# Column products three steps apart and spline ramps two steps apart, in work that runs beside a convolution

## The chip, the cores and the metric

The kernel runs on one core of a Trainium2 chip. The metric is the device time of one execution in microseconds; a kernel's time is the median of several runs. Five engines matter: TensorE (PE, matrix products into PSUM), ScalarE (ACT), VectorE (DVE), GpSimd (POOL) and SyncE (SP), which here only issues transfers between HBM and the core's memory (SBUF). Each engine works through its own instructions in the order in which the program gives them, and semaphores hold an instruction until what it needs is there.

## What is computed

The input x has shape 8 x 64 x 128 x 128, in float32. Four layers follow each other, each after a group norm and each added to its input:

```python
x = x + L0(gn(x))   # adder convolution 3x3: relu(b - sum |patch - w|)
x = x + L1(gn(x))   # per element: scale_base * silu + scale_sp * cubic B-spline + bias
x = x + L2(gn(x))   # Haar transform, depthwise 3x3, pointwise, 3x3, gelu, inverse Haar
x = x + L3(gn(x))   # nearest of 512 embedding vectors per pixel
```

Layer 0 costs most: for each of 64 output channels the absolute difference of every input channel and tap is formed and summed over 64 channels and 9 taps. Group norm needs a whole image before the next layer can begin.

## The kernel before

Images are worked on in pairs: 2 images x 64 channels fill the 128 partitions. There are four pairs. **Layer 0** (`layer0`) of a pair is 4 chunks of 32 rows x 4 groups of 16 output channels, 16 passes; each pass has 16 x 9 = 144 *taps*. A tap is one of three things. ScalarE forms |x - w| for a whole chunk (L821, 128 x 4096 elements). Or VectorE forms a maximum (L774), which gives the absolute difference with terms added elsewhere. Or VectorE fuses a second maximum into the same buffer (L844). TensorE then sums the buffer over the channels with 8 matmuls of 512 columns (L809), and the buffer is free again. There are seven narrow buffers, and beside the other layers two wide ones that also hold the padded input.

The order is written out ahead by a planner, when the program is built. It keeps a clock for each engine, adds a fixed cost for each instruction (`COSTS`, `ABS`, `MAX`, `FUSED`, `SUM`), and always issues what can start first. The number of taps for each engine in a pass follows from its clocks.

**Beside** layer 0 of the pairs 1, 2 and 3 run layers 1, 2 and 3 of the pair before (`layer1_beside`, `layer2_beside`, `layer3_beside`). They are cut into *steps*. `STEPS` gives how many steps each layer has (208, 500, 24 for the first statistics of a later pair, 396), 1128 in all for a pair's 16 x 144 = 2304 taps, so that a step comes about every second tap. `at(step, f, ...)` lists what is issued in which step; within a step the order is that of the listing. The planner knows what these pieces cost, but no waits between them. Layers 1 to 3 of the last pair run alone at the end; the change does not touch them.

**Layer 1 beside** takes 16 chunks a pair, one in 12 steps. For each of three knots p and two images i: a ramp (`ramp_on_act`, ScalarE, L1340, for three of the six; else `ramp`, VectorE, L1345), its square (ScalarE, L1349) and its cube (VectorE, L1353), then `products` (TensorE, L1368, 8 matmuls) of both images. Ramps have two buffers, squares and cubes three (`r3`), used in turn: a ramp waits until the cube two before has read its buffer, a square until the products have read the buffer of three before. `silu`, `base`, `right` (L1377) and `total` (L1381, L1382) end a chunk. With the chunk's first step b and s = b + 1 + 4p, the ramps of both images are in step s, the squares in s + 1, the cubes in s + 2, the products in s + 4.

**Layer 2 beside** takes 8 chunks a pair, one in 56 steps. Four *kinds* of column products m follow each other. `columns_of` (VectorE, L1496) makes the input `v`; four *bursts* of 12 matmuls (`products`, TensorE, L1511) fill `mm`; a *take* moves `mm` out of PSUM into even and odd columns of `g`. The tiles `v`, `mm` and `g` have one buffer each. Each burst has its own weights, `u2`, 384 KB, loaded by SP (`load_u2`) into one buffer: the load can go when the burst before has read the buffer. SP issues this load among others: rows of x (L1451, L1558), results (L1574, L673). `gelu` (ScalarE, L1551), `inverse` (TensorE, L1564), `add` (VectorE, L1569) and `store` follow.

With b the chunk's first step, kind m has `columns_of` in step b + 11m, its bursts in b + 11m + 3, 5, 7 and 9, its take in b + 11m + 11. GELU is in b + 46, the inverse products in b + 48, 49, 57 and 58. The takes are:

```python
first:  ScalarE  even = mm               # kind 0
second: VectorE  even += mm              # kind 1, L1536
        ScalarE  odd   = mm              #         L1537
third:  VectorE  even += mm; odd -= mm   # kind 2, L1542, L1543
fourth: VectorE  odd  -= mm              # kind 3, L1547
```

In the second take both engines write the same tile `g`, and the copy waits for the addition.

Of the kernel before, what the change touches and what calls it, by code (L numbers as in the profile page):

```python
# [16 lines left out]
ALU = mybir.AluOpType  # L17
# [22 lines left out]
PADDED = (RA + 2) * (W + 2)  # L40
ALONE = (9, 3, 9.0, 9.0, 11.0, 54)
BESIDE = (7, 99, 7.0, 8.0, 10.0, 40)
STEPS = (208, 500, 24, 396)
ABS_ALONE = [60] * NP
ABS_BESIDE = [66, 66, 66, 70, 73, 74, 74, 74, 74, 72, 68, 66, 66, 66, 66, 66] * 3
FIRST_MAX = 3
# [22 lines left out]
    "layer2_beside.border": {"DVE": 0.4},  # L69
    "layer2_beside.columns_of": {"DVE": 1.42},  # L70
    "layer2_beside.products": {"PE": 2.95},
    "layer2_beside.take_first": {"ACT": 1.0},
    "layer2_beside.take_second": {"DVE": 1.18, "ACT": 1.0},
    "layer2_beside.take_third": {"DVE": 2.36},
    "layer2_beside.take_fourth": {"DVE": 1.18},
    "layer2_beside.gelu": {"ACT": 1.05},
# [22 lines left out]
class Net:  # L99
# [1191 lines left out]
    def layer1_beside(self, pair, stats_in, stats, steps):  # L1291

        nc, tc = self.nc, self.tc
# [5 lines left out]
        def at(step, f, *a):  # L1299
            events[step].append((f, *a))  # L1300

        with ExitStack() as ctx:
# [89 lines left out]
            for n in range(2 * NCH):  # L1392
                b = 12 + EACH * n
                for i in range(2):
                    at(b - 2, load, n, i)
                    at(b, magnitude, n, i)
                at(b - 1, load_x, n)
                for p in range(NQ // 2):
                    s = b + 1 + 4 * p
                    for i in range(2):  # L1400
                        at(s, ramp_on_act if p < 1 + i else ramp, n, p, i)
                        at(s + 1, square, n, p, i)
                        at(s + 2, cube, n, p, i)
                    at(s + 4, products, n, p)
                at(b + 5, silu, n)
                at(b + 9, base, n)
                at(b + 14, right, n)
                at(b + 15, total, n)
            yield from self.spread_out(events, steps)

    def layer2_beside(self, stats_in, stats, steps):
# [3 lines left out]
        nc, tc = self.nc, self.tc  # L1415
# [6 lines left out]
        def at(step, f, *a):  # L1422
            events[step].append((f, *a))

        with ExitStack() as ctx:
# [96 lines left out]
            def even_and_odd(c):  # L1522
                g = gs[c].rearrange("p o i r (w b) -> p b i o (r w)", b=2)
                return g[:, 0], g[:, 1]

            def product_of(c, m):
                return mms.pop((c, m)).rearrange("p i o r w -> p i o (r w)")

            def take_first(c):
                gs[c] = sp.tile([P, 2, 2, G, S], F32, name="g")  # L1530
                nc.scalar.copy(even_and_odd(c)[0], product_of(c, 0))

            def take_second(c):
                even, odd = even_and_odd(c)
                ps = product_of(c, 1)
                nc.vector.tensor_tensor(even, even, ps, ALU.add)  # L1536
                nc.scalar.copy(odd, ps)  # L1537

            def take_third(c):
                even, odd = even_and_odd(c)  # L1540
# [38 lines left out]
            for j in range(NCH + 1):  # L1579
                b, each = (7, LEAD) if j == 0 else (7 + LEAD + EACH * (j - 1), EACH)  # L1580
                if j < NCH:
                    lo, row = (2 * G * j + 4, 2) if j else (0, 0)
                    hi = min(2 * G * (j + 1) + 4, H)
                    for h, s in enumerate((-5, -2, 1, 4) if j else range(0, 10, 2)):
                        to = min(lo + G // 2, hi)
                        if lo == to:
                            continue
                        at(max(b + s - 3, 0), load, j, h, lo, to)
                        at(b + s + 1, columns, j, h, to - lo)
                        if h == 0 and j > 0:  # L1590
                            at(b + s + 2, halo, j)
                        at(b + s + 2, rows, j, h, to - lo, row)
                        row += (to - lo) // 2
                        lo = to
                    for n in range(36):
                        at(b + 7 + n * (each - 10) // 36 if j else b + 11 + n * (each - 14) // 36, depthwise, j, n)
                    at(b + each - 2, border, j)
                if j >= 1:
                    c = j - 1
                    when = [(b + 11 * m + 3 + 2 * n, c, m, n // 2, n % 2) for m in range(4) for n in range(4)]  # L1600
                    for n, (step, *what) in enumerate(when):
                        at(when[n - 1][0] + 1 if n else b - 3, load_u2, *what)
                        at(step, products, *what)
                    for m, take in enumerate((take_first, take_second, take_third, take_fourth)):
                        at(b + 11 * m, columns_of, c, m)
                        at(b + 11 * m + 11, take, c)
                    for oab in range(2):
                        at(b + 46, gelu, c, oab)
                    for a in range(2):
                        s = b + 48 + 9 * a  # L1610
                        at(s - (8 if a == 0 else 1), load_x, c, a, 0)
                        for n in range(2):
                            at(s + n, inverse, c, 2 * a + n)
                        for h in range(2):
                            for n in range(2):
                                at(s + 3 + 4 * h, add, c, 2 * a + n, h)
                            at(s + 3 + 4 * h, store, c, a, h)
                        at(s + 4, load_x, c, a, 1)
# [101 lines left out]
    def run(self):  # L1720
# [5 lines left out]
        def raw(pair):  # L1726
            mrs[pair] = self.mr_tile()
            return self.raw_norm(pair, mrs[pair])

        def beside():  # L1730
            for pair in range(last):
                later = self.stats_tile("later")
                yield from self.layer1_beside(pair, stats.pop(pair), later, STEPS[0])
                between = self.stats_tile("between")
                yield from self.layer2_beside(later, between, STEPS[1])
                if pair + 1 == last:
                    self.load_early(last)
                if pair + 2 <= last:
                    yield from self.padded(raw(pair + 2), STEPS[2])
                yield from self.layer3_beside(between, pair, STEPS[3])  # L1740

        self.layer0([0], mrs, stats, ALONE, ABS_ALONE, [0] * (NP - 2) + [STEPS[2], 1], self.padded(raw(1), STEPS[2]))
        counts = []
        for pair in range(1, last + 1):
            total = sum(STEPS) + (1 - STEPS[2] if pair == last else 0)
            lead = 0 if pair == 1 else 20
# [49 lines left out]
```

## Time and profile before

| what | value |
| --- | --- |
| median of 3 runs | 18329.01 us (18328.6 to 18329.49) |
| profiled execution | 18391.41 us |
| its span | 18389.7 us |
| granted clock of TensorE, mean | 0.985 |
| busy: PE, DVE, ACT, POOL | 97%, 96%, 93%, 18% |
| layer 0 of the first pair, alone | about 0 to 3600 us |
| the three stretches beside layer 0: layer 1 | 3640 to 4545, 8280 to 9170, 12840 to 13725 us |
| layer 2 | 4545 to 6580, 9170 to 11150, 13725 to 15720 us |
| layer 3 | 6690 to 8200, 11260 to 12750, 15770 to 17270 us |
| layers 1 to 3 of the last pair, alone | about 17390 us to the end |

The profiled execution is 62 us longer than the median of the runs, so a sum over its rows is a difference that is then carried to the median. A row of the profile names a line of the code, an engine, an operation, the tile written and the tiles read; `r` stands for the ramps and for `r3` alike, `u` for `u2` and for the `u` of layer 1 (numbers in names are left out). A wait is written as "who <- for whom: total, how often, the longest", in us. PE busy times are modelled at their ends; idle gaps of an engine under 150 ns are not listed as waits. Each of the program's matmuls stands as two records.

### The profile page before, as it was taken

How to read it: one execution, taken by the hardware profiler on the slowest of the kernel's cores; microseconds unless marked ns; L12 is line 12 of the kernel's file. 1: busy time of each engine (PE TensorE's matmuls, PEld its weight loads, DVE VectorE, ACT ScalarE, POOL GpSimd, SP SyncE). 2: the span in 40 equal slices, each digit the busy share in tenths (PEclk: the TensorE clock that was granted, in tenths of full speed). 3: DMA queues.
4: the chain of work that ended last, by engine and by line, in shares of the span. 5: the costliest groups of instructions: out<-in, count | busy, mean ns of one | idle time of the engine just before them, and what ended most of it. 6: DMA issues, size and time to landing. Idle time of an engine off the chain costs nothing.

```text
span 18389.7 us, 338059 instructions
## 1 busy us (share of the span) xinstructions
PE 17822.3 (97%) x150418; PEld 6142.1 (33%) x150418; DVE 17676.9 (96%) x13410; ACT 17162.3 (93%) x6556; POOL 3386.7 (18%) x1866
## 2 busy tenths in 40 slices
PE   8999999999999999999999999999999999999998
PEld 2222222222333323332233333233223333222364
DVE  8999999999999999999999999999999999999887
ACT  7999999999999999999999999999999999999924
POOL 1222222200000024430000002443000000344205
PEclk9999999999999999999999999999999999999997
DMA  7767777611111111011111111101111111110231
GB/s 146 132 124 137 132 130 137 130 40 40 43 48 49 44 39 26 23 31 38 41 41 48 53 43 39 29 23 29 42 39 44 45 53 43 28 28 21 66 107 42
DMA packets 454213, 1099.90 MB, mean 60 GB/s; under 512 B 72416, under 2 KB 234848, under 8 KB 395360
## 3 DMA queue, kind: packets, MB, share of 16 engines
q0 software_dynamic: 111792, 491.89, 15.2%
q1 hardware_dynamic: 340960, 586.39, 11.2%
q8 instruction: 1178, 19.30, 0.4%
q14 instruction: 283, 2.32, 0.0%
HBM read 526.58 MB, written 125.74 MB: 35 GB/s over the span
## 4 chain that ended last, share of the span: by engine, by line
PE 54%; DVE 26%; issue 11%; ACT 6%; DMA 2%; POOL 1%; SPq 0%; DVEq 0%; another core or an unknown queue 0%; ACTq 0%; POOLq 0%
PE ps L809 41%; DVE buf L774 13%; ACT buf L821 4%; PE mm L1511 4%; DVE buf L844 4%; PE pd L1666 2%; DVE r L1353 1%; DVE wide L774 1%; PE ps L1227 1%; PE m L1079 1%; DMA u<-u_dram 1%; DVE dw L1484 1%; DVE nd L1678 1%; DVE x L774 1%; PE pa L953 0%
## 5 line engine op out<-in xcount | busy, mean ns | idle before, releaser
L809 PE MATMUL ps<-buf,sel 128*32 128x512 f32 x112848 | 12574.1, 595 | 168.4 <-ACT buf L821 87.6
L821 ACT ACTIVATE buf<-wide,w 128x4096 f32<-128x4096 f32 x1901 | 6922.4, 3711 | 80.1 <-PE ps L809 79.3
L821 ACT ACTIVATE buf<-x,w 128x4096 f32<-128x4096 f32 x1823 | 6647.1, 3711 | 129.3 <-PE ps L809 123.6
L809 PEld LDWEIGHTS ps<-buf,sel 128*32 128x32 f32 x112848 | 3540.5, 110 | 8634.0 <-issue 7801.0
L774 DVE TENSOR_SCALAR buf<-x,w 128x4096 f32<-128x4096 f32 x1801 | 4166.2, 2357 | 75.2 <-PE ps L809 68.8
L774 DVE TENSOR_SCALAR buf<-wide,w 128x4096 f32<-128x4096 f32 x1731 | 4028.8, 2367 | 95.3 <-PE ps L809 89.7
L1681 POOL DMA_INDIRECT g<-in_L_conv_embed_weight,ix x768 | 1860.2, 2422 | 2390.0 <-issue 1170.8
L844 DVE SCALAR_TENSOR_TENSOR buf<-x,w,buf 128x4096 f32<-128x4096 f32 x440 | 1973.3, 4485 | 15.7
L658 POOL DMA_DIRECT2D y<-in_x x496 | 704.9, 2173 | 6961.4 <-ACT y L645 5343.3
L844 DVE SCALAR_TENSOR_TENSOR buf<-wide,w,buf 128x4096 f32<-128x4096 f32 x430 | 1928.4, 4485 | 15.3
L1511 PE MATMUL mm<-v,u 64*128 64x256 f32 x9216 | 1182.0, 401 | 142.1 <-DMA u<-u_dram 129.1
L1511 PEld LDWEIGHTS mm<-v,u 64*128 64x128 f32 x9216 | 893.4, 195 | 557.4 <-issue 239.3
L832 POOL DMA_DIRECT2D buf<-buf x203 | 508.0, 2503 | 2739.6 <-DVE buf L774 2363.2
L821 ACT ACTIVATE x<-wide,w 128x4096 f32<-128x4096 f32 x263 | 975.9, 3711 | 5.8 <-PE ps L809 5.8
L821 ACT ACTIVATE wide<-x,w 128x4096 f32<-128x4096 f32 x259 | 961.1, 3711 | 4.8 <-PE ps L809 4.8
L809 PE MATMUL ps<-wide,sel 128*32 128x512 f32 x7696 | 923.1, 594 | 11.4 <-ACT wide L821 4.6
L809 PE MATMUL ps<-x,sel 128*32 128x512 f32 x7776 | 927.2, 593 | 3.3 <-ACT x L821 1.9
L1484 DVE SCALAR_TENSOR_TENSOR dw<-sub,dws,dw 128x512 f32<-128x512 f32 (+2 forms) x768 | 573.4, 747 | 10.4
L1668 ACT ACTIVATE t<-emb,xsq 128x512 f32<-128x512 f32 x768 | 512.2, 718 | 42.3 <-DVE xsq L1659 23.8
L1678 DVE CUSTOM_DVE_ANT_0 nd<-pd,t 128x512 f32<-128x512 f32 x768 | 519.6, 677 | 32.5 <-ACT t L1668 17.0
L774 DVE TENSOR_SCALAR x<-wide,w 128x4096 f32<-128x4096 f32 x223 | 529.5, 2374 | 8.9 <-PE ps L809 8.8
L1680 DVE FIND_INDEX8 ix<-best,nd 128x8 uint32<-128x512 f32 x768 | 526.2, 685 | 0.0
(288 smaller groups left out, 10465.5 us busy)
## 6 DMA issues: line engine op xcount, KB each, us to landing
buf<-buf POOLq DMA_DIRECT2D x203, 2048.0 KB
u<-u_dram SPq DMA_DIRECT2D x512, 384.0 KB
z<-x_dram SPq DMA_DIRECT2D x192, 256.0 KB
x<-x_dram SPq DMA_DIRECT2D x96, 512.0 KB
raw<-in_x SPq DMA_DIRECT2D x32, 1024.0 KB
x_dram<-y SPq DMA_DIRECT2D x512, 64.0 KB
y<-in_x POOLq DMA_DIRECT2D x496, 64.0 KB
x_dram<-x SPq DMA_DIRECT2D x48, 512.0 KB
```

The lines of the kernel that those rows point to most:

```text
L658: nc.gpsimd.dma_start(out=ys[p][at], in_=d, accum_op=ALU.add)
L774: nc.vector.tensor_scalar(ab, tap(p // OG, t), w[:, t : t + 1], None, ALU.max)
L809: nc.tensor.matmul(to, sel[:, M - 1 - m : 3 * M - 1 - m], rhs, start=(done % TAPS == 0), stop=((done + span) % TAPS == 0))
L821: nc.scalar.activation(ab, tap(p // OG, t), AF.Abs, bias=w[:, t : t + 1], scale=-1.0)
L832: nc.gpsimd.dma_start(out=into, in_=of, accum_op=ALU.add, max_dma_last_dim=8192)
L844: nc.vector.scalar_tensor_tensor(ab, tap(p // OG, t), w[:, t : t + 1], ab, ALU.max, ALU.add)
L1484: nc.vector.scalar_tensor_tensor(out, v, wt, out, ALU.mult, ALU.add)
L1511: nc.tensor.matmul(ps[:, i], u2[r, k % 2, di, :], vs[c, m][r, k, di : di + G, :], start=(k == 0 and di == 0), stop=(k == 3 and di == 2))
L1668: nc.scalar.activation(t, emb[:, 1], AF.Identity, bias=xsqs[j][:, n : n + 1])
L1678: nc.vector.tensor_tensor_reduce(nd, ps, t, 1.0, -FAR, ALU.subtract, ALU.max, mx[:, 0:1])
L1680: nc.vector.max_index(ix, mx, nd)
L1681: nc.gpsimd.indirect_dma_start(out=g[:, img, :], out_offset=None, in_=self.embed, in_offset=bass.IndirectOffsetOnAxis(ap=ix[:, 0:1], axis=0),)
```

## The change

In layer 1 beside, the ramps, squares and cubes of the second image are issued two steps after those of the first, and the cube two steps after its square; the products come in step s + 7. What ends a chunk comes three steps later. In layer 2 beside, the bursts stand three steps apart and the kinds 14 steps; a take is in the 15th step after its `columns_of`. Kind 1 is worked on first, and its take is two copies by ScalarE, into even and odd columns; kind 0 is second and only adds to the even columns. GELU and what follows move to b + 58 and b + 60. The steps of a chunk stay 12 and 56. The step counts grow from 208 to 212 and from 500 to 514, so that 1146 steps fall on the same 2304 taps. Buffers are as before.

```diff
-STEPS = (208, 500, 24, 396)
+STEPS = (212, 514, 24, 396)
...
-    "layer2_beside.take_first": {"ACT": 1.0},
-    "layer2_beside.take_second": {"DVE": 1.18, "ACT": 1.0},
+    "layer2_beside.take_first": {"ACT": 2.0},
+    "layer2_beside.take_second": {"DVE": 1.18},
...
                 for p in range(NQ // 2):
                     s = b + 1 + 4 * p
                     for i in range(2):
-                        at(s, ramp_on_act if p < 1 + i else ramp, n, p, i)
-                        at(s + 1, square, n, p, i)
-                        at(s + 2, cube, n, p, i)
-                    at(s + 4, products, n, p)
-                at(b + 5, silu, n)
-                at(b + 9, base, n)
-                at(b + 14, right, n)
-                at(b + 15, total, n)
+                        at(s + 2 * i, ramp_on_act if p < 1 + i else ramp, n, p, i)
+                        at(s + 2 * i + 1, square, n, p, i)
+                        at(s + 2 * i + 3, cube, n, p, i)
+                    at(s + 7, products, n, p)
+                at(b + 8, silu, n)
+                at(b + 12, base, n)
+                at(b + 17, right, n)
+                at(b + 18, total, n)
...
             def take_first(c):
                 gs[c] = sp.tile([P, 2, 2, G, S], F32, name="g")
-                nc.scalar.copy(even_and_odd(c)[0], product_of(c, 0))
+                ps = product_of(c, 1)
+                for to in even_and_odd(c):
+                    nc.scalar.copy(to, ps)
 
             def take_second(c):
-                even, odd = even_and_odd(c)
-                ps = product_of(c, 1)
-                nc.vector.tensor_tensor(even, even, ps, ALU.add)
-                nc.scalar.copy(odd, ps)
+                even = even_and_odd(c)[0]
+                nc.vector.tensor_tensor(even, even, product_of(c, 0), ALU.add)
...
                     c = j - 1
-                    when = [(b + 11 * m + 3 + 2 * n, c, m, n // 2, n % 2) for m in range(4) for n in range(4)]
+                    kinds = ((1, take_first), (0, take_second), (2, take_third), (3, take_fourth))
+                    when = [(b + 14 * at_m + 3 + 3 * n, c, m, n // 2, n % 2) for at_m, (m, _) in enumerate(kinds) for n in range(4)]
                     for n, (step, *what) in enumerate(when):
                         at(when[n - 1][0] + 1 if n else b - 3, load_u2, *what)
                         at(step, products, *what)
-                    for m, take in enumerate((take_first, take_second, take_third, take_fourth)):
-                        at(b + 11 * m, columns_of, c, m)
-                        at(b + 11 * m + 11, take, c)
+                    for at_m, (m, take) in enumerate(kinds):
+                        at(b + 14 * at_m, columns_of, c, m)
+                        at(b + 14 * at_m + 15, take, c)
                     for oab in range(2):
-                        at(b + 46, gelu, c, oab)
+                        at(b + 58, gelu, c, oab)
                     for a in range(2):
-                        s = b + 48 + 9 * a
+                        s = b + 60 + 9 * a
```

## The prediction

> **What bounds the kernel now.** I read the first part of the page, then a table of stretches, then the waits of each stretch, then the timeline at two of the waits.
>
> ```profile
> span 18389.7 us, 338059 instructions
> PE 17822.3 (97%) x150418; PEld 6142.1 (33%) x150418; DVE 17676.9 (96%) x13410; ACT 17162.3 (93%) x6556; POOL 3386.7 (18%) x1866
> ```
>
> Three engines are nearly full, so the kernel is a ring: ScalarE and VectorE each fill a buffer with one tap, TensorE sums it, the buffer comes free. No single engine bounds it; a wait costs time when it runs round this ring. The table of stretches (window, length, then busy time of PE, PEld, DVE, ACT, POOL) shows where the ring loses, for the first pair that runs beside the convolution: its layer 1, its layer 2, its layer 3.
>
> ```profile
> 3640.00:4545.00 905.00, 878.32 (x6840) 260.35 (x6836) 870.22 (x474) 873.86 (x386) 23.04 (x17) 0.99 0.14 39
> 4545.00:6580.00 2035.00, 1958.97 (x17168) 755.79 (x17164) 1945.25 (x1194) 1937.95 (x572) 89.97 (x73) 0.98 0.17 46
> 6690.00:8200.00 1510.00, 1504.54 (x12840) 455.63 (x12840) 1491.23 (x1530) 1502.59 (x649) 689.51 (x305) 1.00 0.11 26
> ```
>
> Layer 3 idles 5 to 19 us per engine, layer 1 some 27 to 35, layer 2 76 to 97. The change touches the two losing stages. Over the three pairs layer 1 takes 2680 us and layer 2 6010 us; TensorE's idle time there is 27 + 40 + 23 = 90 and 76 + 70 + 62 = 208 us.
>
> The Trainium skill, "Perfetto Trace Analysis", section Identifying the Most-Contended Engine, warns that matmul busy time is a poor measure of headroom. The start times agree: a sum of 16 records starts 1.717 us after the last one where nothing waits, and by that TensorE lost some 8% of the layer 2 stretch and not the 4% that its busy time leaves; by the rule there would be more to gain than I count.
>
> The waits of the second pair's layer 2 (engine, line, what it waited for: total, times, longest):
>
> ```profile
> ACT buf L821 <- PE ps L809: 55.5, 33, 6.8
> PE mm L1511 <- DMA u<-u_dram: 47.6, 15, 6.5
> DVE buf L774 <- PE ps L809: 46.8, 24, 6.7
> ACT g L1537 <- DVE g L1536: 33.3, 8, 8.0
> ```
>
> TensorE waits for the weights of the column products (one `u2` buffer), and ScalarE and VectorE then wait for TensorE by the same amount: that wait is on the path. One of them in the timeline:
>
> ```profile
> 9345.00 0.32 SPq L1451 DMA_DIRECT2D xin<-x_dram  x1
> 9345.41 10.29 SPq L1500 DMA_DIRECT2D u<-u_dram  x2
> 9349.00 1.22 PE L1511 MATMUL mm<-v,u 64*128 64x256 f32 x4 [4.18 <-DMA u<-u_dram]
> 9357.32 7.32 ACT L821 ACTIVATE buf<-x,w 128x4096 f32<-128x4096 f32 x2 [6.78 <-PE ps L809]
> ```
>
> The burst before ended at 9339.5, but SP stood at another load until 9345.0; the weights left at 9345.4, TensorE idled 4.18 us, and 8 us later ScalarE lacked a buffer for 6.78 us.
>
> **Part 1, bursts three steps apart.** A step in layer 2 is 228.5 / 56 = 4.08 us (chunk period over its steps); the longer step counts (1128 to 1146 for the same 2304 taps) make it 4.02. A load takes 2.86 us from issue to its last packet (median of 360), and its issue follows the former burst by 0.04 us where SP is free, by up to 10 us where it is not. Between bursts the program had a median of three sums (5.15 us), two in a tenth of the cases; after the change five (8.58 us), at least three. The wait is 129.1 us in 42 pieces on TensorE, 142 us in 50 with those booked under another name. Taking 4.02 us off each leaves 16 pieces with 16 us. More loads than before stand behind other SP transfers (148 against 92 of 360), so I keep 25 us: gain 129 - 25 = **104 us**, bounds 0 (SP's queue moves the waits along) and 142.
>
> What comes late next: the copies out of the single `mm` now begin 15 steps after the chunk's start, one later than needed by the old pattern, and the next burst follows in two steps and not three. In the old trace the next burst starts 4.9 us (second kind) and 5.7 us (third) after the take ends, mean of 24. One step less leaves 0.9 and 1.7, plus 1.2 for the second, whose ScalarE copy is gone. A quarter of 72 bursts then waits 1 to 2 us: **-30 us**, bounds 0 and -90 (72 adds of 1.25 us fully exposed); behind such a burst stand TensorE's sums, and both producers lack buffers. The first take has two copies (2 x 1.15 us) but had 10.1 us to spare; no cost (28 us if that cover went). The Trainium skill ("Perfetto Trace Analysis", Matmuls) wants independent matmul groups to rotate through PSUM banks so that copying out overlaps the next group; this speaks against a change that keeps one `mm` and closes the gap. By the rule all 72 takes would be exposed, the upper bound, and the sum would be 60 us worse.
>
> **Part 2, second kind first.** The same two copies and four VectorE operations per chunk, so no work is added. Gone: ScalarE's wait for VectorE's add (L1537, 96.1 us in 23 pieces) and, with take three steps after the burst, its wait for the burst (L1531, 22.3 us). New: GELU follows the last take by one step, not two; it started 3.5 us after it, so -0.5 now, about 1.5 us of waiting in each of 24 chunks, 36 us, with ScalarE's taps queued behind. Net 82 us of ScalarE. In these stages ScalarE also waits 142 us for buffers, so its own waits are mostly hidden behind TensorE's; I count **15 us**, bounds -10 and 60. The next chunk's first copy must wait for the last inverse product; it had 40.7 us and loses eight steps (32 us): free.
>
> Layer 2: 104 - 30 + 15 = **89 us gained**, bounds -100 and +200.
>
> **Part 3, ramps two steps apart.** Step here: 17.8 us between product bursts over 4 = 4.45 us. Work is unchanged. Three gaps move. The cube waits for its square by two steps, not one (VectorE's 38.3 us at L1353 go). A ramp reuses its buffer one step after the cube that frees it, not two (ScalarE's 67.3 us at L1340 would grow). And the square of the second image takes the buffer (three of them) that the products of the *same* step free; it had one step. The tight spot can be seen once already:
>
> ```profile
> 3957.98 1.08 PE L1368 MATMUL pa<-r,l1w 128*64 128x512 f32 x4
> ...
> 3961.72 1.06 ACT L1349 ACTIVATE r<-r 128x1024 f32<-128x1024 f32 x1 [2.02 <-PE pb L1368]
> ```
>
> The square at L1349 stands until the burst is over. Today squares start 4.7 us after it on average. ScalarE work that belongs to the same step as a burst reaches its place 3.7 us (first ramps of the next chunk, 45 cases) to 5.2 us (third ramp, 48) before the burst ends: that is the new wait, 141 times. Behind it on ScalarE are its taps, for which TensorE waits. They now lie ready 3.1 us before TensorE wants them (shortest in a cycle, mean of 140). So 0.6 to 2.1 us a time get through, 85 to 300 us. Counted in the changed order, cycle by cycle: ScalarE's path from the burst's end (square 1.045, taps 3.711) against TensorE's work until it wants each tap (sums 1.717); ScalarE is late in 66% of 138 cycles, 1.43 us on average, 197 us in all; in the old order 0.10 us, 13 us. The ramps' longer wait lies inside this one, since the next square would have to wait anyway.
>
> This does not add up in full: the old cycle is 17.82 us for 16.63 of TensorE work, 1.19 of it waiting (164 us). New floor: 16.43 + 1.43 = 17.86, as long as the old cycle. If a third of the old waits stay on top: **+50 us**, bounds -40 (taps absorb it, VectorE's 38 us count) and +184 (all of it on top).
>
> **Sum.** 50 - 89 = -39 us, and the counts of sums (8020 to 8018) and fused maxima (993 to 995) are worth 4 us each on two engines, one with each sign. I take **-40 us**. The profiled execution took 18391.4 us, 62 above the runs' median of 18329.0; I carry the difference over: 18351 profiled, **18289 us** median.
>
> **Rivals.** (B) The ring's slack takes up the square's wait, and with bursts spread over 51 of a chunk's 56 steps instead of 39 ScalarE's 82 us count too: -104 - 60 - 0, some -160 us, 18170. For it: layer 2's taps lie ready 8.5 us. Against: layer 1's only 5. (C) SP's queue merely moves the `u2` waits, or takes replace them: the change does not do what it says; 0 to -10 us, 18325. For it: 148 loads behind others. (D) Slower: ScalarE's square stands in line 141 times for the products of its own step, in layer 1, with old waits on top: +184 - 89 = +95 us, 18425. It decides from the point where taps lie ready less than the 3.7 to 5.2 us; their shortest are 3.1 on average, which speaks for it.
>
> **Chances.** Forecast 0.42 (0.28 of it more than 0.2%, or 37 us, below; a run of this kernel can hardly tell less from no change), B 0.22, C 0.12 (0.02 faster, 0.08 same, 0.02 slower), D 0.24 (0.22 slower). Faster 0.52, same 0.24, slower 0.24. The range from 18170 to 18440 cuts B's lower and D's upper half. The forecast's own is 18235 to 18330.
>
> **What would show it.** The wait of L1511 for `u` should fall from 129 to some 25 us, those at L1531 and the old L1537 to none, new ones of L1511 for takes stay near 30. In layer 1 the wait of L1349 for L1368 should rise from 6.7 us to over 150 and L1353's for L1349 nearly vanish. I am wrong if layer 2's stretches do not shrink by some 30 us a pair, or layer 1's grow by over 60 or shrink.

## The result and the profile after

The changed kernel takes 18371.1 us, median of 12 runs (18363.7 to 18384.9), the kernel before 18329.3 us (18320.4 to 18334.3): ratio 1.0024, 95% interval 1.0015 to 1.0033. It is 42 us slower. I had forecast 40 us faster; the time lies inside the range, on the wrong side.

The profiled execution of the changed kernel has a span of 18365.7 us, shorter than the 18389.7 us of the one before. That is no contradiction: in the execution profiled before, the last stage, whose code is the same, ran at a lower granted clock. From the last ReLU of layer 0 to the end (layers 1 to 3 of the last pair) it took 1115 us there at a mean granted clock of 0.89, and 1064 us here at 0.91; up to that point the changed kernel is 27 us behind. So the two traces are compared by stretches, and the median runs decide the whole.

The first part of the page after, and its table of stretches (window, length, busy PE, PEld, DVE, ACT, POOL, clock, DMA, GB/s) for the first pair's layers 1, 2 and 3:

```profile
span 18365.7 us, 337983 instructions
PE 17789.4 (97%) x150386; PEld 6105.2 (33%) x150386; DVE 17674.5 (96%) x13410; ACT 17164.8 (93%) x6556; POOL 3336.2 (18%) x1866
```

```profile
3640.00:4600.00 960.00, 892.87 (x6868) 252.85 (x6864) 885.85 (x481) 883.73 (x389) 23.43 (x23) 0.99 0.13 37
4600.00:6590.00 1990.00, 1948.48 (x17182) 753.97 (x17178) 1943.84 (x1187) 1929.80 (x570) 81.27 (x67) 0.99 0.17 47
6690.00:8200.00 1510.00, 1489.73 (x12652) 449.19 (x12644) 1482.00 (x1525) 1494.43 (x647) 688.14 (x306) 0.99 0.10 26
```

The busy shares of the whole span do not move; the stretches do, against each other. In layer 1 every engine now idles 67 to 76 us (27 to 35 before), in layer 2 some 42 to 60 (76 to 97 before). A kernel that is nearly unchanged in total has two large changes inside.

Passes of layer 0 give the sizes, since each has the same 144 taps. Passes 15 to 18, 31 to 34 and 47 to 50 (told apart by their ReLUs, counted from 0), in which layer 1 runs beside, took 3513 us before and 3694 after: **181 us lost**. The eight passes after each of these, mostly layer 2, took 6773 and 6624: **149 us won**. (The step counts shift the border between them by some 40 us, as the run with the counts alone shows below, so these two sizes hold only roughly; the runs of each part alone settle them.) Layer 1's loss is 60 us a pair, at the edge of what the prediction named as a sign of being wrong.

Where layer 1 lost, from the waits of the second pair's layer 1 after (who waited for whom: total, times, longest):

```profile
ACT r L1349 <- PE pb L1368: 77.2, 34, 7.0
DVE r L1353 <- ACT r L1349: 70.2, 22, 7.7
PE ps L809 <- ACT buf L821: 65.6, 38, 4.8
DVE buf L774 <- PE ps L809: 20.1, 6, 10.8
```

Read from top to bottom these make one loop: ScalarE's square waits for the products, VectorE's cube for that square, TensorE for the tap that stands behind the square on ScalarE, VectorE for a buffer that TensorE has not freed. Before, the same stretch had 1.5, 24.3, 16.3 and 3.0 us. In the timeline after (start, length, engine, line, operation, and in brackets the idle time before it) the loop can be followed once:

```profile
8593.32 1.03 PE L1368 MATMUL pb<-r,l1w 128*64 128x512 f32 x4
...
8594.38 1.06 ACT L1349 ACTIVATE r<-r 128x1024 f32<-128x1024 f32 x1 [2.76 <-PE pb L1368]
8595.34 2.36 ACT L1336 ACTIVATE z<-z,zb 128x1024 f32<-128x1024 f32 x2
...
8596.19 3.64 PE L809 MATMUL ps<-buf,sel 128*32 128x512 f32 x32
8597.61 7.30 ACT L821 ACTIVATE buf<-x,w 128x4096 f32<-128x4096 f32 x2
...
8601.36 1.06 PE L809 MATMUL ps<-buf,sel 128*32 128x512 f32 x8 [1.53 <-ACT buf L821]
```

The burst ends at 8594.35, and the square starts at 8594.38 after ScalarE has stood for 2.76 us. Behind it come two magnitudes and then the first tap, ready at 8601.3. TensorE has two ready sums (32 records), is through with them at 8599.8 and stands for 1.53 us.

Where layer 2 won, its waits in the second pair after:

```profile
ACT g L1551 <- DVE g L1547: 18.5, 5, 6.7
PE mm L1511 <- DMA u<-u_dram: 15.7, 9, 3.4
ACT g L1533 <- PE py L1564: 9.1, 3, 4.8
ACT buf L821 <- PE ps L809: 8.4, 8, 1.9
...
DVE buf L774 <- PE ps L809: 3.2, 2, 2.4
```

The wait for `u2` fell from 47.6 to 15.7 us, and with it the two waits that the prediction put down to it, ScalarE's and VectorE's for buffers, from 55.5 and 46.8 to 8.4 and 3.2.

### The profile page after: what moved, and what is told of

Same layout as the page of the kernel before. It is cut to its first block, busy times and chain, and to the rows that moved or that the text cites. A ratio compares the mean times of both kernels' runs of the same rounds, so it can differ in the third digit from the quotient of the medians.

```text
span 18365.7 us, 337983 instructions
## 1 busy us (share of the span) xinstructions
PE 17789.4 (97%) x150386; PEld 6105.2 (33%) x150386; DVE 17674.5 (96%) x13410; ACT 17164.8 (93%) x6556; POOL 3336.2 (18%) x1866
## 4 chain that ended last, share of the span: by engine, by line
PE 58%; DVE 23%; issue 9%; ACT 8%; DMA 1%; POOL 0%; SPq 0%; DVEq 0%; ACTq 0%; POOLq 0%
PE ps L809 45%; DVE buf L774 11%; ACT buf L821 6%; DVE buf L844 4%; PE mm L1511 4%; PE pd L1667 2%; DVE dw L1484 1%; PE pa L1368 1%; PE ps L1227 1%; PE m L1079 1%; PE pb L1368 1%; PE py L1564 1%; DVE x L774 1%; ACT wide L821 1%; DVE nd L1679 0%
## 5 line engine op out<-in xcount | busy, mean ns | idle before, releaser
L809 PE MATMUL ps<-buf,sel 128*32 128x512 f32 x112720 | 12599.8, 596 | 263.3 <-ACT buf L821 205.5
L809 PEld LDWEIGHTS ps<-buf,sel 128*32 128x32 f32 x112720 | 3533.3, 110 | 8756.1 <-issue 7718.4
L1511 PE MATMUL mm<-v,u 64*128 64x256 f32 x9216 | 1156.5, 395 | 84.1 <-DMA u<-u_dram 67.6
L821 ACT ACTIVATE x<-wide,w 128x4096 f32<-128x4096 f32 x283 | 1050.2, 3711 | 4.5 <-PE ps L809 4.5
L1511 PEld LDWEIGHTS mm<-v,u 64*128 64x128 f32 x9216 | 878.7, 191 | 490.6 <-issue 307.3
L809 PE MATMUL ps<-wide,sel 128*32 128x512 f32 x7760 | 930.7, 594 | 23.5 <-ACT wide L821 21.6
L809 PE MATMUL ps<-x,sel 128*32 128x512 f32 x7808 | 931.7, 593 | 1.1 <-DVE x L844 1.1
L821 ACT ACTIVATE wide<-x,w 128x4096 f32<-128x4096 f32 x247 | 916.2, 3709 | 3.0 <-PE ps L809 2.8
L774 DVE TENSOR_SCALAR wide<-x,w 128x4096 f32<-128x4096 f32 x238 | 561.3, 2359 | 1.3 <-PE ps L809 1.3
```

The source lines that it names most:

```text
L774: nc.vector.tensor_scalar(ab, tap(p // OG, t), w[:, t : t + 1], None, ALU.max)
L809: nc.tensor.matmul(to, sel[:, M - 1 - m : 3 * M - 1 - m], rhs, start=(done % TAPS == 0), stop=((done + span) % TAPS == 0))
L821: nc.scalar.activation(ab, tap(p // OG, t), AF.Abs, bias=w[:, t : t + 1], scale=-1.0)
L1511: nc.tensor.matmul(ps[:, i], u2[r, k % 2, di, :], vs[c, m][r, k, di : di + G, :], start=(k == 0 and di == 0), stop=(k == 3 and di == 2))
```

## The experiments

My theory after the result: the change is two changes of opposite sign. Layer 1 pays in full for a square that takes a buffer which the products of its own step free, layer 2 gains more than I had said. The rivals: an interaction of the two parts; the longer step counts and the planner's new order; the ramps' shorter reuse instead of the squares'. Times below are differences from the kernel before, run on the same chip in the same set; their intervals are about 16 to 29 us to each side. The whole change stands at +42 us. Versions of different sets are compared by these differences. The traces bear them out: each version's distance from the kernel before up to the last ReLU of layer 0, which leaves the last stage out, is within 19 us of the difference given here.

### The two parts alone, and the square's buffer

`l2_alone` is the layer 2 part without the layer 1 part (steps 208 and 514), `l1_alone` the reverse (212 and 500).

> The layer 2 part alone; layer 1 as before, its steps back at 208. Theory (the two parts pull apart: layer 1 pays in full for squares that wait for the products of their own step, layer 2 gains more than I said): 18329 - 110 to -160, so 18170 to 18220 us, and L1511's wait for u2 at 50 to 70 us. Rival (layer 2's waits are only moved, and what the two traces show there is the phase in which layer 1 leaves the engines): 18310 to 18345 us.

Measured: 18174.6 against 18336.4 us, **-162 us**, ratio 0.9912 (0.9897 to 0.9927). L1511's wait for `u2` 64 us. The theory holds, at the far end of its range.

> The layer 1 part alone; layer 2 as before. Theory: 18329 + 150 to +200, so 18480 to 18530 us, with L1349 waiting some 200 us for L1368 and TensorE waiting over 150 us for ScalarE's taps in the layer 1 stretches. Rival (the slack of the ring takes up most of the wait, and the loss came from elsewhere): 18310 to 18390 us.

Measured: 18538.1 us, **+202 us**, ratio 1.0108 (1.0093 to 1.0124). Over the whole run:

```profile
PE ps L809 <- ACT buf L821: 238.1, 146, 7.6
ACT r L1349 <- PE pb L1368: 236.7, 108, 8.2
DVE r L1353 <- ACT r L1349: 213.9, 72, 9.6
```

-162 and +202 make +40; measured together +42. Within the intervals the two parts add, and the slack of the ring took up little: L1349's wait for L1368 grew by 230 us (from 6.7), the time by 202.

`after_four_squares` gives squares a fourth buffer.

```diff
-                cubes[n, p, i] = sp.tile([P, N], F32, name="r3", bufs=3)
+                cubes[n, p, i] = sp.tile([P, N], F32, name="r3", bufs=4)
```

> The changed kernel with four buffers for squares and cubes and not three: the square of the second image then takes the buffer of the products four steps earlier. Theory: L1349's wait for L1368 falls from 207 us to under 10, and layer 1's loss of 150 to 200 us goes: 18170 to 18220 us. Rival (the ramps' reuse one step after the cube, or the later cubes, cost it): 18340 to 18370 us, with the wait turned up at L1340 or L1368.

Measured: 18233.1 us, **-103 us**, ratio 0.9944 (0.9931 to 0.9958), so 145 us below the whole change, between the two expectations and nearer to the theory's. L1349's wait for L1368 is gone from the list and L1353's for L1349 fell from 178 to 45 us. The buffer is the cause of these 145 us, but 59 us are missing beside `l2_alone`.

`products_early` leaves three buffers and moves the products instead.

```diff
-                    at(s + 7, products, n, p)
+                    at(s + 6, products, n, p)
```

> The changed kernel with layer 1's products in step s + 6, still three buffers: one step again between the products and the square that takes their buffer, but only one between the last cube and the products. Theory (the place of the square decides): L1349's wait for L1368 falls under 60 us, TensorE's wait for cubes rises to 40 to 90 us, 18230 to 18300 us. Rival (reuse of the ramps' buffers): as the changed kernel, 18360 to 18380 us.

Measured: 18182.7 us, **-154 us**, ratio 0.9914 (0.9901 to 0.9928): better than expected. L1349's wait for L1368 is 12.6 us, and the wait that I thought would replace it, L1368 for cubes, did not rise (29.7 us, 25.8 in the changed kernel). One line of the schedule is worth nearly 200 us, 51 us more than the fourth buffer.

### What in layer 2 pays, and the step counts

`steps_only` changes `STEPS` and nothing else; `swap_only` takes the kinds in the new order with the new takes, but two steps apart; `spacing_only` has the layer 2 part of the change with the old order of kinds and the old takes.

> The kernel before with the changed step counts alone (212 and 514), no instruction moved between steps: every step is 1.6% shorter, and the planner writes a new order. Theory (the counts are only length): 18310 to 18350 us. Rival (layer 2's gain, or layer 1's loss, comes from the denser steps and the new order): under 18290 or over 18370 us.

Measured: 18330.4 against 18336.0 us, **-6 us**, ratio 0.9996 (0.9987 to 1.0005). The counts, and with them a wholly new planned order, are worth nothing in sum. (In its trace the layer 1 passes took 41 us more and the layer 2 passes 42 us less: the border moves.)

> The kernel before with kind 1 first and its two ScalarE copies in one take; bursts two steps apart as before. Theory (TensorE's wait for u2 carries layer 2): L1537's 96 us go but ScalarE waits longer for buffers, L1511's wait for u2 stays at 110 to 150 us, 18280 to 18330 us. Rival (ScalarE's wait for VectorE's addition carries a good part): 18230 to 18270 us.

Measured: 18311.8 us, **-24 us**, ratio 0.9985 (0.9976 to 0.9994). ScalarE's wait at the old second take (96 us) is gone, but its waits for buffers of all three kinds rose from 214 to 265 us and those of its ramps at L1340 from 67 to 93: most of its freed time went into other waits, as expected while TensorE waits for `u2` (120 us).

> Layer 2 with bursts three steps apart and the longer step count, but the kinds in their old order, with the copy that waits for the addition; layer 1 as before. Theory: most of the layer 2 part's 162 us, 18180 to 18240 us, with L1537's wait still 70 to 130 us. Rival: half of the gain or less, 18250 to 18310 us.

Measured: 18183.3 us, **-153 us**, ratio 0.9916 (0.9902 to 0.9929). Its waits over the whole run:

```profile
ACT buf L821 <- PE ps L809: 113.0, 92, 12.9
DVE buf L774 <- PE ps L809: 84.1, 61, 14.8
PE mm L1511 <- DMA u<-u_dram: 76.0, 34, 5.5
...
ACT g L1537 <- DVE g L1536: 62.1, 17, 8.8
```

The three steps carry the layer 2 part: 153 of 162 us, with ScalarE's second take still waiting. But TensorE's wait for `u2` fell only from 129 to 76 us. The start times show where more was won, though not why. From first to last burst, all three pairs: before 5267 us for 2132 sums, here 5227 us for 2167 sums, 2.47 and 2.41 us a sum, or some 125 us for 2150 sums. TensorE's listed idle time there fell from 168 to 103 us, the bursts, from the first record's start to the last one's, from 2.71 to 2.63 us each (30 us for 384), and what is left of the 125 us must lie in gaps too short to be listed.

`after_three_ramps` has a third buffer for ramps, squares as in the changed kernel.

```diff
-                rs[n, p, i] = sp.tile([P, N], F32, name="r", bufs=2)
+                rs[n, p, i] = sp.tile([P, N], F32, name="r", bufs=3)
```

> The changed kernel with three buffers for ramps and not two, squares still three. Theory (squares decide, ramps' waits lie inside theirs): L1340's wait for L1353 goes from 38 us to under 5, L1349's for L1368 stays at 180 to 240 us, 18340 to 18375 us. Rival (the ramps' reuse costs the 60 us by which four buffers for squares fell short of the layer 2 part alone): 18300 to 18330 us.

Measured: 18364.0 us, +28 us, ratio 1.0015 (1.0006 to 1.0024); beside the whole change's +42 no difference that the intervals hold. L1340's wait is gone, L1349's for L1368 is 231 us. The ramps' buffers are not the cause.

### Another cure, and what is left

`square_late` moves the second image's square instead of the products.

```diff
-                        at(s + 2 * i + 1, square, n, p, i)
+                        at(s + 3 * i + 1, square, n, p, i)
```

> The changed kernel with the square of the second image one step later (s + 4 and not s + 3), products still in s + 7, three buffers: the square follows the products that free its buffer by one step again, and nothing else moves. Theory (that one place decides): L1349's wait for L1368 falls from 207 us to under 60, 18180 to 18250 us. Rival (the late products themselves, s + 7, cost layer 1 its time): 18300 us or more.

Measured: 18361.4 against 18396.8 us, **-35 us**, ratio 0.9981 (0.9972 to 0.9990). The theory failed in its number, and 18361 us lies in the rival's range. The wait for the products did fall, to 19 us, but others took its place:

```profile
DVE r L1353 <- ACT r L1349: 127.5, 39, 8.5
PE ps L809 <- ACT buf L821: 114.1, 73, 8.0
ACT r L1340 <- DVE r L1353: 87.6, 44, 8.0
...
ACT r L1349 <- DVE r L1345: 63.6, 23, 6.2
```

The cube now follows its square by one step, and the next ramp follows the cube by one: ScalarE to VectorE and back in two steps. Three runs beside it try whether more buffers are worth something where the square has its step, and which version is best.

`early_three_ramps` is `products_early` with a third buffer for ramps.

> Products in s + 6 and three buffers for ramps. Theory: with the square's place mended, ramps' waits (41 us at L1340) are no longer hidden in it and count a little: 18140 to 18180 us, L1340's wait under 5. Rival (they were never on the path): 18175 to 18195 us.

Measured: 18235.3 us, -162 us, ratio 0.9910 (0.9896 to 0.9923). Without the third buffer it was -154, and L1340's 41 us are gone. Counted from 18329 us, the theory allowed 149 to 189 us below the kernel before and the rival 134 to 154; the intervals can't tell 8 us, so the run doesn't decide between them. Most of the 41 us were hidden behind other waits.

`early_four_squares` is `products_early` with a fourth buffer for squares.

> Products in s + 6 and four buffers for squares. Theory: the place in the order has removed nearly all of the wait (13 us left), so the fourth buffer is worth nothing more: 18165 to 18195 us. Rival (squares' buffers still hold ScalarE): under 18150 us.

Measured: 18239.0 us, -158 us, ratio 0.9910 (0.9895 to 0.9925), beside -154 with three buffers. As the theory has it (its absolute time is not, since this chip gave 18397 us to the kernel before): with the place in the order right, the buffer is worth nothing that can be told.

This run shows one thing more. It differs from `after_four_squares` only in the step of the products, s + 6 and not s + 7, and stands at -158 us where that one stands at -103. No square waits for products in either. So the late products cost some 55 us of their own, of which the traces have 39 in the passes of layer 1 and 16 in the eight after each. By which wait they do it, or whether through the order that the planner then writes, is not shown; VectorE's wait for the products at L1377 is 21.0 us with the late ones and 0.4 with the early ones, L1340's 71 and 41.

`l2_three_ramps` is `l2_alone` with a third buffer for ramps.

> The layer 2 part alone with three buffers for ramps, layer 1's order as before. Theory: L1340's wait for L1353 (61 us) goes and a part of it counts, 18130 to 18170 us. Rival (hidden behind other waits): 18165 to 18185 us.

Measured: 18227.6 us, -169 us, ratio 0.9906 (0.9891 to 0.9921), beside -162 with two. No difference that can be told, and L1340 still waits 47 us for cubes: inconclusive. It is the lowest ratio of all, but five other versions lie within 16 us of it.

Three last runs ask what is left of layer 1's loss. `l1_four_squares` is `l1_alone` with a fourth buffer for squares.

> The layer 1 part alone with four buffers for squares; layer 2 as before. Theory (the square's wait is all of layer 1's loss; the 60 us by which four buffers fell short of the layer 2 part alone came mostly with the new order in layer 2): +0 to +35 us on the kernel before, against +202 with three buffers. Rival (the two-step ramps cost layer 1 another 50 us by themselves): +40 to +80 us.

Measured: 18406.3 against 18400.0 us, **+6 us**, ratio 1.0004 (0.9995 to 1.0013), against +202 with three buffers. The fourth buffer takes away all of layer 1's loss. That need not mean that the square's wait was the only cost: a gain of the spread ramps can cover another one, as the next run shows. Of the 59 us by which `after_four_squares` fell short of `l2_alone`, the traces have 35 us in the passes of layer 1 and 23 us in the eight after each.

`l1_early` is `l1_alone` with the products in s + 6.

> The layer 1 part alone with products in s + 6, three buffers; layer 2 as before. Theory: within 25 us of the kernel before, L1349's wait for L1368 under 25 us. Rival (the spread of the ramps is worth something once the square is free): 30 us or more below it.

Measured: 18350.1 us, **-50 us**, ratio 0.9974 (0.9963 to 0.9984). Here the rival holds: alone, the spread ramps are worth something once the square is free. With the layer 2 part they are not (`products_early` -154, `l2_alone` -162), so here the parts do not add. Beside `l1_four_squares`, where no square waits for products but these stand in s + 7, it is 56 us faster, much what the late products cost above, and here both were run in one set. Its layer 1 passes take as long as before and its layer 2 passes 46 us less, but the border between them moves with the counts; where the 50 us come from stays open.

`late_three_ramps` is `square_late` with a third buffer for ramps.

> The kernel with the late square (s + 4) and three buffers for ramps. Theory (the late square only moved the tight place: between ScalarE's square and VectorE's cube, and between that cube and ScalarE's next ramp, one step each, a round of two crossings in too little time; a third buffer loosens the second): L1340's wait for L1353 falls from 88 us to under 15, L1353's for L1349 from 128 to under 70, the time 100 to 160 us below the kernel before, against 35 with two buffers. Rival (the late square itself is the cost): 20 to 60 us below it.

Measured: 18308.7 us, **-91 us**, ratio 0.9948 (0.9935 to 0.9962), between the two expectations. L1340's wait is gone, L1353's for L1349 fell from 128 to 70 us, the layer 1 passes by 58 us. The same buffer bought 8 us in `products_early`. So the tight round of square, cube and ramp is part of what the late square costs. Some 70 us remain beside `l2_alone`. The late products (s + 7), which `square_late` and this run keep, would account for 55 of them; no run moves them here, and L1349's wait for VectorE's ramps (84 us) is left too.

## Why the prediction was wrong

**The failed step** is the sum of part 3: "If a third of the old waits stay on top: +50 us". Alone, this part measured +202 us. The mechanism was right and the new wait about as long as counted: the prediction had ScalarE late by 197 us in all, 184 more than in the old order, and the trace after shows 207.5 us at L1349 (6.7 before) and 205.5 us of TensorE waiting for ScalarE's taps (87.6 before). What was wrong is that I let the new wait displace the old ones; no row stood behind the "third". I set a floor ("16.43 + 1.43 = 17.86, as long as the old cycle") and took it for nearly the answer.

The cycle itself, from one burst of layer 1's products to the next (mean of 141), shows what came instead: 17.82 us before with 7.13 sums in it, 18.87 us after with 7.02. By the prediction's own figures for TensorE's work, 16.63 and 16.43 us, what is not work rose from 1.19 to 2.44 us, by 1.25. All of the new lateness on top would be 1.33 (1.43 less 0.10). So nearly all of the old waiting stayed, and not a third. The floor had a second fault: the 0.20 us of work by which its cycle is shorter are not saved. The same 2304 taps have to be summed, and these sums, some 28 us in 138 cycles, fall to other stretches.

Single waits on the ring went both ways. L1340's fell from 67 to 38 us and L1368's for cubes from 41 to 26, but VectorE's for the square grew nearly as much as the new wait itself, because a late square makes the cube late as well:

```profile
ACT r L1349 <- PE pb L1368: 207.5, 99, 7.0
PE ps L809 <- ACT buf L821: 205.5, 126, 7.6
DVE r L1353 <- ACT r L1349: 178.4, 61, 10.5
```

The last line is the second error: "VectorE's 38.3 us at L1353 go" and "nearly vanish". I gave the cube two steps after the square's *place* in the order; ScalarE stood at that place for up to 7.0 us. The bound named "all of it on top", +184 us, was nearly the answer, and rival D's mechanism the true one; its point of decision (taps ready less than 3.7 to 5.2 us) had been met by the prediction's own 3.1. D's total, +95 us, was missed because layer 2 won more than the 89 us that D took over.

**Part 1** had the right mechanism and was too small. `u2`'s wait fell to 67.6 us, not 25; the queue behind other transfers did matter, with 78 of 360 loads leaving over 1 us late after and 49 before. Yet three steps won 153 us where I had 104 - 30. The sum counted one listed wait. In `spacing_only` ScalarE's and VectorE's waits for buffers fell with it, by 90 and 74 us over the run, the bursts were shorter, and some 30 us more must lie in gaps too short to be listed; which of these the spread bursts win directly is not shown.

The 30 us for the next burst waiting for the take came out at 16. The list of waits does not name a take: it books six bursts under "issue" (15.1 us) and three under "PE ps L809" (1.3 us). But each of these nine starts 0.10 us after a VectorE operation that reads `mm` has ended (L1537, L1543 or L1547). The longest is this:

```profile
6452.47 1.22 DVE L1543 TENSOR_TENSOR g<-g,mm 128x1024 f32<-128x1024 f32 x1
...
6453.79 1.23 PE L1511 MATMUL mm<-v,u 64*128 64x256 f32 x4 [5.30 <-issue]
```

Seven of the nine are among the 72 that the prediction counted. By **the rule on PSUM banks** (the Trainium skill, "Perfetto Trace Analysis", Matmuls) all 72 takes would have been exposed; the trace shows a small part of that, since two steps between take and burst were enough for the other 65.

**Part 2** was right in kind: `swap_only` gained 24 us where I counted 15, and on top of the three steps it was 9 (162 against 153), which the intervals can't tell from nothing; L1531's wait for the burst is gone; GELU waits 44 us (36 forecast). "Free" was wrong for the next chunk's first copy: it waits 33 us for the inverse product, in 11 pieces, though 8.7 us were to be left on average.

**The ramps' wait** lies inside the square's, as I said: L1340's fell from 67 to 38 us, and a third buffer changed nothing. **The sum** missed by two errors of opposite sign: layer 1 cost 152 us more than counted (202 against 50), layer 2 won 73 us more (162 against 89). -40 was forecast, +42 measured; that the time lies inside the range is luck: with layer 2 as counted it would have been some 18442 us.

## What to carry to other kernels

In a ring of full engines in which each engine's order is fixed, count a new wait nearly in full: an engine that stands for another's last instruction is late with all that is queued behind it. Here 230 us more of one wait cost 202 us. A path count gives a floor, not a forecast; the price was nearer to the floor's wait added on top of the old ones. When a schedule is spread out with the same buffers, look for every buffer whose release and reuse now fall into the same step. Here one line moved by one step was worth nearly 200 us, and a buffer more 145 of them. A cure can make the next place tight: with the square moved and not the products, square, cube and ramp followed each other by one step each between two engines, and most of the loss stayed. And look at what started just before a waiting instruction when a list books its wait under no one.

## What the runs showed of the hardware

The same last stage, from the last ReLU of layer 0 to the end, took 1061 to 1064 us in some traces, at a mean granted clock of 0.91 to 0.92, and 1115 to 1134 us in the others, at 0.88 to 0.89. In its last 400 us the granted clock switches between half and full, with 13 to 15 stretches of half clock in the first kind and 19 to 23 in the second; its mean was 0.83 in the last 372 us of `l2_alone` and 0.75 in the last 429 us of `l2_three_ramps`, both in layer 3 of the last pair. The kernel before took 18336 us in the first two sets and 18397 and 18400 in the others; the traces of the first two sets are all of the first kind, those of the others all of the second. A trace of one execution should be compared stretch by stretch for this reason, and versions by their difference from the kernel before in the same set.
